# Image sums in four column tiles, an energy split in halves, and half of the attention additions moved behind the roots, in a two-layer kernel on Trainium2

## The chip, the cores and the metric

The kernel runs on one core of one Trainium2 chip, all in float32. The metric is the device time of one launch in microseconds (us), compared between kernels that are timed on the same chip. The kernel before takes 2922.1 us in the median of three runs (2920.12 to 2923.42).

## The reference, cut to what matters

`x` holds 4 sequences (B) of 32 images (T) of 128 x 128. Layer 0 normalises x in groups, treats each of the 32 slices of a sequence as an image and runs a neural operator on it: Fourier-based q, k and v with 32 heads, softmax attention over the 32 images, a projection `p`, and then

```python
a = _inorm(p + xa, attn_w, attn_b)
an = _inorm(a, norm2_w, norm2_b)
m = _fno_layer(an, m0cw, m0sw, H, W, inner_norm=True, act=True)
m = _fno_layer(m, m1cw, m1sw, H, W, inner_norm=True, act=False)
out = _inorm(m, mon_w, mon_b) + a
```

`_inorm` subtracts an image's mean and divides by its standard deviation. `_fno_layer` adds a spectral convolution (a product with weights on 64 x 33 Fourier modes) to a scaled copy of its input; with `inner_norm` the convolution's result is normalised first, and `act` puts a gelu behind it. Layer 1 is an additive attention over 1024 tokens and a mixture of experts; the change doesn't touch it.

## The kernel before, in words

Layer 0 is a loop over the sequences, `for b in range(B)` (from L912), with one pass per b of some 193 us. Its instructions are written in program order for a scheduler that decides the order on each engine; `behind(later, earlier)` (L144) adds a dependence that only orders two instructions. Layer 1 (from L1897) has its order written out by hand.

The stage around the change, in one pass:

- `stats` (L258) turns the statistics of `q` (the attention's projected output plus the input, for 32 images) into a mean and a variance per image; its copy to `flat` (L282) also carries the zero mode. The roots are taken by `inv_std` (L243 on): Ln and Exp on ScalarE (ACT; L248, L251), then four small steps on VectorE (DVE; L252 to L255). From them come `ra`, the factor of q in `a`, and `r2`.
- `spectra` (L1101) transforms 32 images to modes in two halves of 16. In each half TensorE (PE) forms `pz` (L305), DVE or ACT copies it to `z` (L225, L227), PE forms `px` (L1123); ACT squares px (`sqx`, L1125); DVE multiplies px with the weights (`part1`, L1134, and `part2`, L1137); GpSimd (POOL) adds the two into `spec` (L1140); ACT writes a negated copy of a part of it (`negative`, L1085). `part1` and `part2` share a ring of three buffers with the `v1` copies (L356).
- `energy` (L1087) weighs the squares (L1091) and sums them over a row (L1099). For layer 0's first convolution it is called once over both halves by `weighed` (L1150), which makes `v0_s`, has PE sum it over the partitions (`ms`, L383) and copies the result (L1169). `inv_std("r0", ...)` and some small DVE steps then make the scale and the bias of the gelu.
- `row_products` (L334) multiplies one half's `spec` with the inverse transform's columns (`y`, 64 matmuls). `inverse_of` has ACT copy y to `v1` (L356) and PE transform it (`four`, L358). `gelu` (L1208 on) adds q in DVE (`g`, L1212), applies the gelu in ACT (L1216; the first one needs another function table, which is loaded there) and takes statistics in DVE.
- `image_rows` (L389) forms, for the *next* sequence, the sums of x and of x squared over the rows of each image: 32 matmuls (L401, 128 x 512 with 32 columns of weights) that accumulate in `rows8`. x goes to partitions 0 to 31, x squared to 32 to 63, so PE uses two column groups. ACT copies `rows8` (`ev`, L410) and `image_moments` (L413) finishes with 8-row matmuls against an identity. It is called once at the start and once in each of the passes b = 0 to 2; `ms` is ordered behind one of its matmuls, the row products behind its last.
- `add_attention` (L1076) forms `a` in place of x with 8 DVE instructions (L1079) a call, one per image, four calls a pass: 32 instructions, 128 in all. They depend on `q` and `ra` only, and are needed at the pass's end. In the text they come behind the gelus, but having no close consumer they are put by the scheduler wherever DVE is found free.
- `coefficients` (L1274 on) makes the final scales of the pass from two more energies and two roots (`r1`, `rm`). In passes b = 0 to 2 `spectra_of_images` (L482) interleaves it with the preparation of the next sequence's images, where `normed[4]` is the last step of that sequence's scales.

## Time and profile before

| view | what | value |
|---|---|---|
| runs | median of 3 | 2922.1 us |
| the profiled execution | its own time, its span, PE's granted clock | 2926.9 us, 2925.1 us, 0.982 |
| layer 0, layer 1 | stretches of the span | 0 to 835.6 us, 835.6 to 2925.1 us |
| busy share | PE, DVE, ACT, POOL | 94%, 75%, 79%, 70% |
| L1079 | 128 instructions, median of one | 0.341 us |
| L1134, L1137 at b=1 | DVE products of one half | 0.69, 0.68 us |
| L1091, L1099 at b=1 | first energy over 1024 elements | 1.21, 1.21 us |
| L401 at b=1 | 32 image sums, from the first to the end of the last | 365.53 to 373.67 us |
| first gelu | b = 0, 1, 2, 3 | 188.37, 379.89, 571.54, 768.25 us |

The profile is of one execution; its times are read against its own span, and only differences carry over to the median. An engine's busy share is a mean over two very different layers. In a time line a row gives start, duration, engine, line, operation, output and inputs, and in brackets the idle time of the engine just before with the instruction that ended it. Instructions on one engine can overlap by some tenths of a microsecond in these records, so that a chain of equal instructions advances by less than one duration each.

### The profile page before, as it was taken

Reading aid. Unit: us, or ns where it says so; the run is one execution under the profiler, and the core shown is the slowest. Engines: PE = TensorE matmul, PEld = TensorE weight load, DVE = VectorE, ACT = ScalarE, POOL = GpSimd, SP = SyncE. Lnnn points to the kernel's source line nnn. Section 1 sums busy time; section 2 is a strip of 40 time slices with the busy share of each in tenths; the row PEclk is TensorE's granted clock in tenths of the full one; section 3 lists DMA queues with packets and bytes.
Section 4 is the critical chain, followed back from the end, with each engine's and each line's share of the span. In section 5 each row is a group of like instructions: output and inputs, shape, how many; then the busy total and the mean of one; then the engine's idle time right before and its main releaser. Section 6 shows DMA issues by size and latency. Waiting matters only on the chain.

```text
span 2925.1 us, 52645 instructions
## 1 busy us (share of the span) xinstructions
PE 2735.4 (94%) x19506; PEld 1352.7 (46%) x19506; DVE 2189.4 (75%) x4860; ACT 2322.9 (79%) x3243; POOL 2034.0 (70%) x1804
## 2 busy tenths in 40 slices
PE   8898998988878999999899999989999999999997
PEld 5565664655544444334444443434444343444443
DVE  4888788778756777666587787657778776878877
ACT  3556466455469999899899999989999998999991
POOL 1706418146139887878988887898787889798773
PEclk9999999999979999999999999999999999999998
DMA  3304205033020101011000100210000011000000
GB/s 101 123 1 112 78 15 163 13 75 101 19 77 9 25 8 33 8 33 41 19 8 17 24 15 17 49 27 14 24 17 15 19 48 26 15 19 15 15 15 15
DMA packets 151152, 107.71 MB, mean 37 GB/s; under 512 B 36302, under 2 KB 140017, under 8 KB 150897
## 3 DMA queue, kind: packets, MB, share of 16 engines
q1 hardware_dynamic: 147633, 102.26, 13.1%
q8 instruction: 154, 2.52, 0.4%
q10 hardware_dynamic: 3264, 2.10, 0.3%
q14 instruction: 101, 0.83, 0.1%
HBM read 63.86 MB, written 19.50 MB: 28 GB/s over the span
## 4 chain that ended last, share of the span: by engine, by line
PE 47%; POOL 11%; ACT 9%; issue 5%; DVE 5%; DMA 0%; POOLq 0%; SPq 0%; DVEq 0%; ACTq 0%
PE d L1854 20%; PE po L1873 12%; PE px L1760 6%; ACT r L1904 5%; PE n L1854 4%; POOL e L1913 3%; POOL e L1912 3%; ACT e L1920 2%; POOL kx L1519 1%; DVE r L1909 1%; DVE xc L1764 1%; POOL x L1519 1%; PE pl L1738 1%; POOL u L989 1%; ACT r L1916 1%
## 5 line engine op out<-in xcount | busy, mean ns | idle before, releaser
L1909 DVE TENSOR_TENSOR r<-n,r 128x1024 f32<-128x1024 f32 (+1 forms) x1056 | 962.0, 953 | 481.5 <-PE n L1854 397.9
L1912 POOL TENSOR_TENSOR e<-r 128x512 f32<-128x512 f32 x528 | 673.2, 1275 | 273.3 <-DVE r L1909 272.8
L1904 ACT ACTIVATE r<-d 128x1024 f32<-128x1024 f32 (+1 forms) x1056 | 792.9, 802 | 67.4 <-PE n L1854 59.3
L1916 ACT ACTIVATE r<-r 128x1536 f32<-128x1536 f32 x528 | 783.6, 1484 | 16.8
L1913 POOL TENSOR_TENSOR e<-e,r 128x512 f32<-128x512 f32 x528 | 671.3, 1271 | 41.4
L1854 PE MATMUL d<-qe,ke 32*128 32x512 f32 (+3 forms) x2304 | 607.5, 603 | 39.9 <-ACT r L1904 35.8
L1873 PE MATMUL po<-e,kx 128*128 128x512 f32 (+3 forms) x1152 | 594.3, 605 | 17.2 <-POOL e L1925 17.2
L1854 PE MATMUL n<-qe,ke 32*128 32x512 f32 (+3 forms) x2304 | 607.0, 602 | 0.0
L1854 PE MATMUL n<-qf,kf 32*128 32x512 f32 (+3 forms) x2304 | 553.5, 555 | 0.0
L1854 PE MATMUL d<-qf,kf 32*128 32x512 f32 (+3 forms) x2304 | 551.9, 555 | 0.0
L1764 DVE SCALAR_TENSOR_TENSOR xc<-px,wgt,xc 128x128 f32<-128x128 f32 x1024 | 358.4, 351 | 41.4 <-PE px L1760 10.6
L1920 ACT ACTIVATE e<-e 128x512 f32<-128x512 f32 x528 | 325.8, 617 | 66.0 <-POOL e L1913 65.1
L1873 PEld LDWEIGHTS po<-e,kx 128*128 128x128 f32 x1152 | 175.4, 188 | 394.6 <-issue 308.6
L1854 PEld LDWEIGHTS d<-qe,ke 32*128 32x128 f32 x2304 | 177.0, 184 | 360.2 <-ACT r L1904 340.2
L1854 PEld LDWEIGHTS d<-qf,kf 32*128 32x128 f32 x2304 | 220.7, 186 | 177.2 <-issue 164.5
L1760 PE MATMUL px<-we,x2t 128*128 128x512 f32 x512 | 265.9, 605 | 6.8 <-DVE xc L1764 5.5
L989 POOL TENSOR_TENSOR u<-xb,gb 128x858 f32<-128x858 f32 (+1 forms) x112 | 220.5, 2008 | 42.6 <-PE po L926 38.8
L1854 PEld LDWEIGHTS n<-qf,kf 32*128 32x128 f32 x2304 | 228.4, 185 | 18.9 <-issue 11.2
L1140 POOL TENSOR_TENSOR spec<-part,part 128x512 f32<-128x512 f32 x16 | 25.8, 1610 | 286.5 <-DVE gn_r_t L253 93.1
L993 DVE TENSOR_TENSOR u<-xw,gb 128x858 f32<-128x858 f32 (+1 forms) x208 | 215.4, 1100 | 6.8 <-ACT xw L980 3.2
L1854 PEld LDWEIGHTS n<-qe,ke 32*128 32x128 f32 x2304 | 177.9, 183 | 9.4 <-DVE r L1909 0.9
L926 PE MATMUL po<-u,pr 128*32 128x429 f32 (+1 forms) x1280 | 151.2, 532 | 24.9 <-POOL u L989 18.5
(425 smaller groups left out, 3378.4 us busy)
## 6 DMA issues: line engine op xcount, KB each, us to landing
xb<-xd SPq DMA_DIRECT2D x128, 214.5 KB
xc<-x SPq DMA_DIRECT2D x29, 512.0 KB
x<-x SPq DMA_DIRECT2D x16, 512.0 KB
qf<-qe SPq DMA_DIRECT2D x64, 128.0 KB
out<-xc SPq DMA_DIRECT2D x15, 512.0 KB
x<-in_x SPq DMA_DIRECT2D x14, 512.0 KB
xb<-xd SPq DMA_DIRECT2D x32, 198.0 KB
kf<-ke SPq DMA_DIRECT2D x32, 128.0 KB
```

The costliest lines, as they stand in the source:

```text
L989: weighed = nc.gpsimd.tensor_tensor(u, xb, gk, ALU.mult)
L993: weighed_last = nc.vector.tensor_tensor(u, xw, gk, ALU.mult)
L1760: nc.tensor.matmul(px, x2t[:, k * P : (k + 1) * P], we[:, e0 : e0 + 4], start=True, stop=True)
L1764: nc.vector.scalar_tensor_tensor(xc[:, k], px[:, e], wgt[:, k, e0 + e : e0 + e + 1], xc[:, k], ALU.mult, ALU.add)
L1854: nc.tensor.matmul(o, k, q, start=turn == 0 or g > 0, stop=turn == 1 or g > 0)
L1873: nc.tensor.matmul(sums[c, h][:, q0 : q0 + c1 - c0], kx[:, jb], e[:, c0:c1], start=jb == 0, stop=is_last and q0 > 2 * P, skip_group_check= ...
L1904: nc.scalar.activation(r[:, g], d, AF.Ln, scale=1.0 / DSCALE)
L1909: nc.vector.tensor_tensor(r[:, g], part, r[:, g], ALU.mult)
L1912: nc.gpsimd.tensor_tensor(e, r[:, 1], r[:, 2], ALU.add)
L1913: nc.gpsimd.tensor_tensor(e, e, r[:, 0], ALU.add)
L1916: nc.scalar.activation(r, r, AF.Exp, scale=-1.0)
L1920: nc.scalar.activation(e, e, AF.Exp)
```

## The change

Five things change in layer 0.

1. `image_rows` uses four column groups: images of even and odd groups of four go to different 32 partitions, for x and for x squared (`rows8` has 128 partitions). `image_moments` adds the two parts by 64-row matmuls against a new constant `one_row`, made by two DVE additions at the start. Of the sums, all but the first two groups are ordered behind the row products of the first half.
2. The first energy is taken in each half, inside `spectra`.
3. In the second half, the row products of the first half, the image sums, the energy's end (`weighed`) and `ms` are written ahead of `part1` and `part2`; `part1` is ordered behind the step that makes `v0_s` (`roots["by_t"]`). `ms` is ordered behind an image sum that is the eleventh instead of the third from last in the list.
4. Sixteen of the 32 additions are written directly behind `ra` and ahead of `spectra`, which gives them precedence.
5. The other sixteen are written in `coefficients`, behind `normed[4]` (b = 0 to 2), or directly behind `flat` of the gelu's statistics (b = 3).

```diff
--- before.py
+++ after.py
@@ -195,6 +195,11 @@
     one_of_8 = const.tile([P, 39], F32, name="one_of_8")
     nc.vector.memset(one_of_8, 0.0)
     nc.vector.memset(one_of_8[:, 7:8], 1.0)
+    one_row = const.tile([P, 8], F32, name="one_row")
+    for m, i in ((0, 0), (1, 33)):
+        nc.vector.tensor_tensor(
+            one_row[:, m::2], ident[:, i : i + 8 : 2], ident[:, i + 64 : i + 72 : 2], ALU.add
+        )
     ones = const.tile([P, P], F32, name="ones")
     nc.vector.memset(ones, 1.0)
 
@@ -279,7 +284,7 @@
         for r, part in ((0, rows[:, 64:]), (64, rows[:, :64])):
             nc.tensor.matmul(x0[r : r + 64, 1], part, pk[:, 0], start=True, stop=True)
         flat = small.tile([P, 2, T], F32, name="flat", tag="flat")
-        nc.vector.tensor_copy(flat, x0)
+        roots["flat"] = nc.vector.tensor_copy(flat, x0)
         return mean, var, flat
 
     def half_rows(images, z, last):
@@ -348,6 +353,7 @@
                     )
                     for earlier in ahead:
                         behind(mm, earlier)
+        roots["rows"] = mm
         return wide
 
     def four_images(wide, g, copy, v_ring=dict(tag="v", bufs=3), tag="b"):
@@ -386,10 +392,10 @@
     def one(name, n=1):
         return small.tile([P, n], F32, name=name, tag=name)
 
-    def image_rows(xt):
+    def image_rows(xt, earlier=None):
 
         products = []
-        rows8 = ps.tile([64, 4, C], F32, name="rows8", tag="a")
+        rows8 = ps.tile([P, 4, C], F32, name="rows8", tag="a")
         for g in GROUPS:
             xx2 = grp.tile([P, GI, C], F32, name="xx2", tag="pr", bufs=6)
             square = nc.scalar.activation(xx2, xt[:, g : g + GI], AF.Square)
@@ -398,15 +404,18 @@
             for h in range(2):
                 m = g // 4 + h
                 for k, src in enumerate((xt[:, 4 * m : 4 * m + 4], xx2[:, 4 * h : 4 * h + 4])):
+                    r = 64 * k + 32 * (m % 2)
                     mm = nc.tensor.matmul(
-                        rows8[32 * k : 32 * k + 32],
+                        rows8[r : r + 32],
                         one_of_8[:, 7 - m : 39 - m],
                         src,
-                        start=m == 0,
-                        stop=m == 7,
+                        start=m < 2,
+                        stop=m > 5,
                     )
+                    if m > 1 and earlier is not None:
+                        behind(mm, earlier)
                     products.append(mm)
-        ev = grp.tile([64, 4, C], F32, name="ev", tag="pr", bufs=6)
+        ev = grp.tile([P, 4, C], F32, name="ev", tag="pr", bufs=6)
         nc.scalar.copy(ev, rows8)
         return ev, products
 
@@ -415,8 +424,8 @@
         s12 = [ps.tile([P, T], F32, name=f"s{t}", tag="a") for t in "ab"]
         for j in range(4):
             for k in range(2):
-                r = slice(32 * k, 32 * k + 8)
-                nc.tensor.matmul(s12[k][:, j::4], ev[r, j], ident[r, r], start=True, stop=True)
+                r = slice(64 * k, 64 * k + 64)
+                nc.tensor.matmul(s12[k][:, j::4], ev[r, j], one_row[r], start=True, stop=True)
         sv = small.tile([P, 2, T], F32, name="sv", tag="sv")
         for k in range(2):
             nc.vector.tensor_copy(sv[:, k], s12[k])
@@ -1073,12 +1082,17 @@
 
         xr = xt
 
-        def add_attention(g):
+        def add_attention(g, earlier=None):
 
             for t in range(g, g + GI):
-                nc.vector.scalar_tensor_tensor(
+                added = nc.vector.scalar_tensor_tensor(
                     xr[:, t], q[:, t], ra[:, t : t + 1], xr[:, t], ALU.mult, ALU.add
                 )
+                if earlier is not None:
+                    behind(added, earlier)
+
+        for g in GROUPS[:2]:
+            add_attention(g)
 
         def negative(spec, slots):
 
@@ -1098,7 +1112,7 @@
                 behind(product, earlier)
             nc.vector.tensor_reduce(s[:, slots], t, AX.X, ALU.add)
 
-        def spectra(layer, src, ready=(), weights=(), earlier=None):
+        def spectra(layer, src, ready=(), weights=(), earlier=None, between=None):
 
             by_re, by_im = layers[layer][:2]
             spec = big.tile([P, GI, 192], F32, name="spec", tag="spec")
@@ -1125,15 +1139,19 @@
                 nc.scalar.activation(
                     sq[:, 0, s4], px.rearrange("p t r x -> p t (r x)"), AF.Square
                 )
-                if a == 0:
+                if a == 0 or layer == 0:
                     for t, by_row in weights:
                         energy(t, sq, by_row, s4, earlier)
+                if a and between is not None:
+                    between(spec, sq)
                 one_, two = (
                     grp.tile(shape, F32, name=n, tag="v", bufs=3) for n in ("part1", "part2")
                 )
-                nc.vector.tensor_tensor(
+                first_part = nc.vector.tensor_tensor(
                     one_, px, by_re.unsqueeze(1).unsqueeze(1).to_broadcast(shape), ALU.mult
                 )
+                if a and between is not None:
+                    behind(first_part, roots["by_t"])
                 nc.vector.tensor_tensor(
                     two, px[:, :, ::-1], by_im.unsqueeze(1).to_broadcast(shape), ALU.mult
                 )
@@ -1161,7 +1179,9 @@
                 s.rearrange("p (k i) -> p k i", i=2).unsqueeze(2).to_broadcast(spread),
                 ALU.mult,
             )
-            nc.vector.scalar_tensor_tensor(by_t, squares, by_column, by_t, ALU.mult, ALU.add)
+            roots["by_t"] = nc.vector.scalar_tensor_tensor(
+                by_t, squares, by_column, by_t, ALU.mult, ALU.add
+            )
             m = sums("ms", ones, by_t, tag)
             if earlier is not None:
                 behind(summing["ms"], earlier)
@@ -1170,13 +1190,21 @@
             return out
 
 
-        spec, sq = spectra(0, q)
-        ahead = []
-        if b + 1 < B:
-            ev, ahead = image_rows(loaded)
-        v0 = weighed("v0", sq, squares, layers[0][2], "a")
-        if ahead:
-            behind(summing["ms"], ahead[-3])
+        sums_of = small.tile([P, GI], F32, name="v0_r", tag="weighed")
+        wide, between = {}, {}
+
+        def energies(spec, sq):
+
+            wide[0] = row_products(spec, 0)
+            ahead = []
+            if b + 1 < B:
+                between["ev"], ahead = image_rows(loaded, roots["rows"])
+            between["v0"] = weighed("v0", sq, squares, layers[0][2], "a", sums_of)
+            if ahead:
+                behind(summing["ms"], ahead[10])
+
+        spec, sq = spectra(0, q, (), [(sums_of, layers[0][2][0])], None, energies)
+        v0 = between["v0"]
         nc.vector.tensor_mul(v0, v0, r2)
         nc.vector.tensor_mul(v0, v0, r2)
         r0, ve = inv_std("r0", v0)
@@ -1190,7 +1218,7 @@
         nc.vector.tensor_tensor(hb, hb, dq, ALU.add)
         gl = big.tile([P, T, C], F32, name=f"g_{b}", tag="y")
         st = grp.tile([P, T, 6], F32, name="st", tag="st")
-        acts, fours, wide = [], {}, {}
+        acts, fours = [], {}
 
         def in_order(act):
 
@@ -1223,9 +1251,8 @@
                 )
                 nc.vector.bn_stats(st[:, t], gl[:, t])
 
-        wide[0] = row_products(spec, 0, ahead[-1:])
         if b + 1 < B:
-            sv = image_moments(ev)
+            sv = image_moments(between["ev"])
         for g in range(4):
             inverse_of(0, g)
         gelu(0, 0)
@@ -1248,14 +1275,14 @@
         in_order(four_rows([gl[:, 8 + t] for t in range(GI)], early[1], 4, nc.scalar.copy))
         if b + 1 < B:
             summed = group_moments(sv, inverted)
-        for g in GROUPS:
-            add_attention(g)
-
         logarithms()
         if b + 1 == B:
             first((ps, images))
 
         glm, glv, flat = stats("gl", st)
+        if b + 1 == B:
+            for g in GROUPS[2:]:
+                add_attention(g, roots["flat"])
         d1, squares = flat_part(1, flat)
         dg = per_image("dq")
         nc.vector.tensor_copy(dg, d1)
@@ -1300,6 +1327,9 @@
             nc.vector.tensor_mul(dg, dg, c3)
             nc.vector.tensor_tensor(cq, cq, dg, ALU.add)
             made["c2"], made["c3"], made["cq"] = c2, c3, cq
+            if product is not None:
+                for g in GROUPS[2:]:
+                    add_attention(g, normed[4])
 
         if b + 1 < B:
             front = spectra_of_images(b + 1, loaded, normed, coefficients)
```

## The prediction

> **What bounds the kernel now.** I read first the page's busy shares and slices, to see which part of the span the change can reach; then the busy table by stage; then the groups and time lines of the one stage that is touched, in the second pass (b=1); last the chain of waits over the same stage in the last pass. Layer 1 starts at 835.6 us and is untouched, so only the first 835.6 us can move, and what moves there shifts the rest by as much.
>
> The stretch that matters runs, in each of the four passes, from the attention weight `ra` (358.72 at b=1) to the first gelu (379.89). Stage table, columns PE, PEld, DVE, ACT, POOL; the rows are this stage, the b=1 stage between the gelus and the next image's fold, and the last pass's tail:
>
> ```profile
> 354.90:379.90 25.00, 24.31 (x248) 15.92 (x247) 23.01 (x88) 13.15 (x26) 3.46 (x2) 1.00 0.01 2
> 397.40:420.80 23.40, 23.04 (x265) 19.94 (x256) 18.95 (x76) 11.93 (x41) 3.01 (x2) 1.00 0.01 2
> 793.90:816.70 22.80, 16.79 (x153) 11.73 (x153) 16.01 (x56) 5.62 (x13) 2.90 (x2) 0.74 0.18 40
> ```
>
> VectorE (DVE) is 92% busy in the first row: no engine has more of its own to do than DVE and TensorE (PE), and both serve one chain. All 32 additions of the pass lie here (group table, b=1, 358.9 to 379.9):
>
> ```profile
> L1079 DVE SCALAR_TENSOR_TENSOR x<-q,ra,x 128x128 f32<-128x128 f32 x32 | 11.2, 372 | 0.0
> ```
>
> Where they stand decides. Time line of DVE, then POOL, then ScalarE (ACT), b=1:
>
> ```profile
> 359.82 0.34 DVE L1079 SCALAR_TENSOR_TENSOR x<-q,ra,x 128x128 f32<-128x128 f32 x1
> 360.55 0.69 DVE L1134 TENSOR_TENSOR part<-px,mask_rows 128x512 f32<-128x512 f32 x1 [0.39 <-ACT sqx L1125]
> 361.15 0.68 DVE L1137 TENSOR_TENSOR part<-px,turned 128x512 f32<-128x512 f32 x1
> 362.19 1.15 DVE L252 TENSOR_TENSOR r_t<-r 128x32 f32<-128x32 f32 x1 [0.35 <-ACT r L251]
> ...
> 364.34 0.68 DVE L227 TENSOR_SCALAR z<-pz 128x512 f32<-128x512 f32 x1
> ```
> ```profile
> 362.01 1.28 POOL L1140 TENSOR_TENSOR spec<-part,part 128x512 f32<-128x512 f32 x1 [37.40 <-DVE part L1137]
> 369.30 2.18 POOL L1140 TENSOR_TENSOR spec<-part,part 128x512 f32<-128x512 f32 x1 [6.01 <-DVE part L1137]
> ```
> ```profile
> 367.07 0.60 ACT L1125 ACTIVATE sqx<-px 128x512 f32<-128x512 f32 x1 [1.31 <-PE px L1123]
> 371.51 0.42 ACT L1085 ACTIVATE spec<-spec 128x256 f32<-128x256 f32 x1 [3.84 <-POOL spec L1140]
> 373.70 0.58 ACT L410 COPY ev<-rows 64x512 f32<-64x512 f32 x1 [1.77 <-PE rows L401]
> 375.81 0.23 ACT L248 ACTIVATE r<-r_ve 128x32 f32<-128x32 f32 x1 [1.53 <-DVE r_ve L247]
> ```
>
> Only three additions precede `part1`; the rest lie behind, among the small steps of the roots. I call T the end of the second square of px (ACT L1125, 367.67): all later steps need it. After T the last to arrive is PE: the image sums end at 373.70 (ACT waits 1.77 for them), only then comes `ms`, then the root, four v copies, a table load and the gelu at T+12.2. In the last pass, which has no image sums, the chain of waits (745 to 769) goes through DVE instead:
>
> ```profile
> 756.01 1.13 DVE sqx L1091
> 757.14 1.27 DVE x L1079
> 758.41 1.13 DVE v_r L1099
> 759.54 0.26 DVE x L1079
> ```
>
> So additions do sit on the path there, five of them in one 1.27 us piece.
>
> **What the Trainium skill says.** "TensorEngine Tiling (Array Packing)", Available Configurations: an array with 128 rows and 32-column tiles holds four tiles that work independently. The trace agrees in kind: 28 records of po L926, four groups, pass in about 3.0 us, 0.107 us each at 429 columns; the image sums in two groups need 0.43 us a pair. "TensorE: Matmul & The Clock Gate", Step-by-step: only weight loads are pulled ahead, matmuls stay in program order. I use it for a y that waits on POOL and holds px behind it; no row of before shows just that. "SBUF — State Buffer", Who interferes with whom: a DVE operation with two SBUF inputs and a POOL operation that reads SBUF exclude each other. The trace agrees: r_t takes 1.15 instead of 0.18 beside the first POOL addition, and the second POOL addition 2.18 instead of 1.28 beside additions of L1079.
>
> **The change part by part.**
>
> **(1) Sixteen additions straight behind `ra`.** The order in which the two built programs stand on each engine has all 16 ahead of the first half's energy and part1 (before: 1, 3, 6 and 0 of them at b=0 to 3). Back to back they are 0.26 us apart, with a small step of the root between them 0.36. From `ra`'s start at 358.72 they and the small steps fill DVE to about 365.2 (16 x 0.36 is 5.8, and some steps more). Then come the new half energy (0.69 + 0.69, some 0.61 apart), part1 and part2: part2 ends at 367.7 instead of 361.83, and POOL adds 367.75 to 369.0 instead of 362.01 to 363.29. The second half's z copy (DVE, was 364.34) now stands behind part2 too, so it ends about 368.5. And the first y of the row products, which waits for POOL, now stands on PE ahead of the last px matmuls; queued behind it are 12 or more px, and ACT's square waits for those. So px runs 369.3 to 370.4 and T is 371.05: **+3.4**. Likewise +4.5 at b=0, +3.0 at b=2, +4.9 at b=3. Bounds: if the block goes at 0.26 throughout, 16 x 0.26 = 4.2 puts part2 at about 366.0 and T at +1.7; nothing, if something else held T anyway.
>
> **(2) From T to the gelu.** Image sums: 32 records at 0.43 a pair are 6.9 us; four wide at 0.107 they are 3.45, and the 24 that stand behind the row products 2.6. Row products (2.07, was on the path after the sums) are done by about T+1.4. The second energy is 512 wide (0.69 each instead of 1.21), and v_s is ready at T+2.0 instead of T+5.9. Sums done T+4.0, so `ms` no longer waits long. DVE: part2 of the second half follows v_s, ending T+3.2 (was T+1.6); POOL T+3.25 to 4.5, now 1.28 since no additions lie beside it; the negation (0.42) to T+4.95; three v copies (1.54) to T+6.45; ev (0.58, now behind them) to T+6.95; Ln, a v copy, Exp to about T+7.85; the DVE steps without additions between, first g at T+9.65, first gelu about **T+10.2 instead of T+12.2**. The following y at PE, for which ACT waits 1.76 before the next v copy (384.83, T+17.16), comes at T+14.8. So -2.4 at b=0 and 1, -1.6 at b=2 (was T+16.4).
>
> Sum at that copy: b=0 +4.5-2.4 = +2.1; b=1 +1.0; b=2 +3.0-1.6 = +1.4. At b=3 no image sums go, but the additions leave the chain (3.1 us of them in the pieces from 757.1 to 767.8) and the wide energy is halved: about -3.8, so +4.9-3.8 = **+1.1** (+0.3 to +1.4). Four passes: **+5.6**.
>
> **(3) The other sixteen, b=0 to 2**: 16 x 0.34 = 5.4 us go to a stage where DVE has 23.40-18.95 = 4.45 us idle and five stand before the coefficients, eleven among them. They need idle times of 0.73, 0.46, 0.88 us there; the xe and xm products, for which the fold waits, move ahead of the rm chain and gain back what the chain loses. I take +0.2 a pass, **+0.6**; bounds -0.5 (xe alone gains) and +2.9 (11 x 0.26, if all are on the path).
>
> **(4) The other sixteen, b=3**: one block behind `flat` (793.95) and ahead of y0, part1 and part2, 16 x 0.26 = 4.2. Hidden: an idle of 0.90 before dq (waits PE d), and part of the 3.08 before the second part1. Layer 1 waits for this tail. I take **+2.4**, bounds 0 and +4.2.
>
> **(5) Start.** The last image's sums pass after its square (14.06); the rows end at 16.0, ev copies, and the pz chain follows. Two more columns take off about half: **-0.8**, bounds -1.2 and 0. The two DVE additions to build `one_row`, about 0.4 us, lie under the first loads: 0; 0.4 if not. The image sums' order against POOL and SP's queue is unchanged.
>
> Sum: 5.6+0.6+2.4-0.8 = **+7.8**. The profiled execution (2926.9; span 2925.1 and 1.8 around it) becomes 2934.7. It lies 4.8 above the runs' median 2922.1; the same sum on the median gives **2929.9**.
>
> **The rivals.**
> - *Wash.* The block costs 1.7 instead of 3 to 5 a pass (0.26 throughout, small steps slip in). For: it is how x5 in 1.27 looks. Against: b=1's interleaved root steps run at 0.36. 7.8-4x1.7 = +1.0: 2923.1.
> - *Gain, the other side.* Mechanism: T doesn't move, because the block fills DVE's wait for r2's root and for px, while the stage after T keeps its gains. Place: part2 L1137 and z L227. Price: -2.4-2.4-1.6-3.8+0.6+2.4-0.8 = -8.0: 2914.1. It decides where T slips under 2.4 us a pass at b=0 and 1. Against: before part1, DVE's only idle is 0.39, and 0.35 behind part2.
> - *The four tiles don't run four wide.* PE then has 24 records in 5.2, `ms` at T+6.7, and ACT is 0.7 to 1 late: +0.9 on three passes, 2932.6; mostly under ACT's copies.
>
> **How the numbers follow.** Forecast 0.50 (its own range 2925 to 2934, from the bounds of 1 and 4), wash 0.22, gain 0.18, narrow tiles 0.10. About 0.2% (5.8 us, 2916.3 to 2927.9) is what a measurement of this kernel tells from no change. Slower: 0.85 of the forecast, all of narrow, 0.15 of wash: 0.56. Faster: 0.7 of the gain, 0.13. Same 0.31. Range 2917 to 2935: it leaves out most of the gain case and the upper end of (3).
>
> **What would show it.** The first POOL L1140 some 8 to 9 us after `ra` (was 3.3); additions at 0.36, sixteen ahead of L1091; PE idle with POOL as releaser before y; the 24 image sums in about 2.6; T to gelu 10.2; at b=3 a block of sixteen behind L282. Wrong if T slips under 2, if the coefficients' chain is pushed 3 us a pass, or if layer 1 starts before 835.6.

## The result, and the profile after

The changed kernel takes 2940.54 us in the median of four runs (2937.82 to 2944.06), the kernel before 2921.68 beside it: the ratio is 1.0063, with a 95% interval of 1.0051 to 1.0075. So it is slower, by 18.9 us; the forecast had +7.8 and a range up to 2935. The direction was right; the forecast size was less than half of the measured one. The profiled execution after is the longest of the four, 2944.06 (span 2942.3).

Layer 1 begins with ScalarE's table load at 835.55 before and at 856.63 after: layer 0 lost 21.1 us in these two executions. Layer 1, the same code, took 2089.6 and 2085.7, and 2083 to 2090 in the runs below; such differences are not of the change. In what follows the stages of layer 0 are compared, since they are steadier than the whole: in runs in which a stage has the same instructions, most of its times agree within 0.1 us. Two stretches are not steady: the start takes 163.3 to 165.8 in the runs with four column tiles and 164.4 to 166.5 in those with two, and `xe` to the next `ra` at b=2 takes 131.3 to 136.8 over all runs, so that the measured changes of these two rows are within their spread.

All times in us. T is the end of the second square of px of a pass, "copy" the next v copy after the first gelus, `xe` the first fold product of the second stage.

| stage | forecast change (b=0, 1, 2, 3) | measured change | sum forecast | sum measured |
|---|---|---|---|---|
| `ra` to T | +4.5, +3.4, +3.0, +4.9 | +6.22, +4.45, +3.13, +7.91 | +15.8 | +21.7 |
| T to the copy | -2.4, -2.4, -1.6, -3.8 | -1.76, -1.98, -1.21, +0.09 | -10.2 | -4.9 |
| copy to `flat` | 0 | -0.01, -0.02, -0.01, 0 | 0 | 0 |
| `flat` to `xe` | +0.2 each | +0.71, +0.67, +0.60 | +0.6 | +2.0 |
| `xe` to the next `ra` | 0 | -0.23, -0.08, -0.17 | 0 | -0.5 |
| last tail, from `flat` | +2.4 | +3.44 | +2.4 | +3.4 |
| start, to the first `ra` | -0.8 | -0.67 | -0.8 | -0.7 |
| all | | | +7.8 | +21.1 |

The block is where it was forecast. DVE's time line at b=1, after (`ra` stands at 362.98 now), then POOL's and PE's:

```profile
364.08 1.40 DVE L1088 SCALAR_TENSOR_TENSOR x<-q,ra,x 128x128 f32<-128x128 f32 x5
...
368.41 1.14 DVE L1088 SCALAR_TENSOR_TENSOR x<-q,ra,x 128x128 f32<-128x128 f32 x4
369.46 0.69 DVE L1105 TENSOR_TENSOR sqx<-sqx,energy 128x512 f32<-128x512 f32 x1
...
371.26 0.68 DVE L1155 TENSOR_TENSOR part<-px,turned 128x512 f32<-128x512 f32 x1
371.86 0.68 DVE L232 TENSOR_SCALAR z<-pz 128x512 f32<-128x512 f32 x1
```
```profile
372.11 1.26 POOL L1158 TENSOR_TENSOR spec<-part,part 128x512 f32<-128x512 f32 x1 [43.16 <-DVE part L1155]
```
```profile
366.57 1.06 PE L1137 MATMUL px<-z,cst 128*32 128x256 f32 x20
...
373.43 0.48 PE L347 MATMUL y<-cst,spec 32*128 32x128 f32 x2 [2.29 <-POOL spec L1158]
373.84 1.89 PE L1137 MATMUL px<-z,cst 128*32 128x256 f32 x24
```

POOL's addition ends 10.39 us after `ra`; the forecast said 10.28. PE then waits 2.29 us at a y for POOL, with the last 24 px behind it, also as forecast. The next row was not: those 24 px take 1.89, though 20 such records took 1.06 seven us earlier. The busy table of stages (seventh number: PE's granted clock) says why:

```profile
370.00:373.40 3.40, 1.07 (x8) 0.16 (x8) 3.40 (x7) 0.02 (x1) 1.26 (x1) 1.00 0.00 0
373.40:378.00 4.60, 4.57 (x78) 3.65 (x82) 2.06 (x7) 1.01 (x2) 0.00 (x0) 0.63 0.00 0
```

PE came out of its wait at half its clock. At b=3 the wait is longer and the half clock lasts. PE's time line there, after, and then the table from the wait to the copy:

```profile
764.50 1.94 PE L1137 MATMUL px<-z,cst 128*32 128x256 f32 x24 [4.22 <-DVE z L232]
766.37 1.65 PE L310 MATMUL pz<-cst,q 128*128 128x128 f32 x6
...
777.72 3.78 PE L364 MATMUL four<-v,cst 128*128 128x512 f32 x4 [2.97 <-ACT v L362]
...
783.41 2.04 PE L364 MATMUL four<-v,cst 128*128 128x512 f32 x2 [0.32 <-DVE g L1240]
```
```profile
764.00:772.20 8.20, 7.70 (x70) 4.86 (x74) 2.54 (x6) 0.97 (x2) 1.27 (x1) 0.50 0.00 0
772.20:774.70 2.50, 2.50 (x58) 2.32 (x54) 2.32 (x5) 0.04 (x1) 0.00 (x0) 0.78 0.00 0
774.70:777.70 3.00, 0.05 (x1) 0.00 (x0) 2.42 (x6) 0.93 (x3) 1.26 (x1) 0.84 0.00 0
777.70:782.00 4.30, 4.29 (x12) 1.75 (x16) 1.29 (x8) 3.06 (x6) 0.00 (x0) 0.50 0.01 4
782.00:790.30 8.30, 7.99 (x68) 4.49 (x60) 6.09 (x26) 3.21 (x9) 0.00 (x0) 0.50 0.00 0
```

In the kernel before, the same stage of b=3 was at half clock from 760.5 to about 767 only. The image sums do run four wide: of the 24 behind the row products, four start every 0.43 us (at b=1 four from 378.44 to 378.46, the next from 378.90 on), where before two did. (These are records: each float32 matmul of the program stands as two records in these traces, so that the "32 matmuls" of the image sums are 16 of the program.)

The tail has the block of sixteen behind `flat`, and nothing hides it except 0.9 us:

```profile
811.59 0.23 DVE L287 COPY flat<-x 128x64 f32<-128x64 f32 x1 [1.17 <-PE x L285]
811.73 4.29 DVE L1088 SCALAR_TENSOR_TENSOR x<-q,ra,x 128x128 f32<-128x128 f32 x16
...
818.76 0.68 DVE L1155 TENSOR_TENSOR part<-px,turned 128x512 f32<-128x512 f32 x1
```

### The profile page after: what moved, and what is told of

Read it like the earlier page. It is cut to its first block, busy times and chain, and to the rows that moved or that the text cites. A ratio compares the mean times of both kernels' runs of the same rounds, so it can differ in the third digit from the quotient of the medians.

```text
span 2942.3 us, 52647 instructions
## 1 busy us (share of the span) xinstructions
PE 2729.9 (93%) x19506; PEld 1347.5 (46%) x19506; DVE 2188.1 (74%) x4870; ACT 2321.8 (79%) x3243; POOL 2033.2 (69%) x1804
## 4 chain that ended last, share of the span: by engine, by line
PE 48%; POOL 14%; ACT 10%; DVE 6%; issue 6%; DMA 0%; POOLq 0%; SPq 0%; DVEq 0%; ACTq 0%
PE d L1884 20%; PE po L1903 11%; PE px L1790 6%; ACT r L1934 5%; POOL e L1942 4%; POOL e L1943 4%; PE n L1884 3%; ACT e L1950 2%; POOL kx L1549 2%; POOL x L1549 2%; DVE r L1939 2%; POOL u L998 1%; DVE xc L1794 1%; PE po L935 1%; PE pl L1768 1%
## 5 line engine op out<-in xcount | busy, mean ns | idle before, releaser
L1884 PEld LDWEIGHTS n<-qf,kf 32*128 32x128 f32 x2304 | 228.0, 185 | 19.3 <-issue 12.2
```

The costliest lines, as they stand in the source:

```text
L1884: nc.tensor.matmul(o, k, q, start=turn == 0 or g > 0, stop=turn == 1 or g > 0)
```

## The experiments

Two theories stood at first. **A**: the block behind `ra` makes the kernel slow, and the rest of the change gains. **B**: the loss is spread over the other parts. A third came from the result: **A2**, that a good part of what the forecast missed is PE's clock, which falls after PE's own idle stretches. Each experiment gives its ratio to the kernel before, timed beside it, with the 95% interval, and then its stages. Medians of different experiments are not compared directly.

### The change without the block

```diff
-        for g in GROUPS[:2]:
-            add_attention(g)
         def negative(spec, slots):
...
+        for g in GROUPS[:2]:
+            add_attention(g)
         logarithms()
```

> The changed kernel without its first step: the first sixteen additions of each pass are written where they were before, behind the gelus, so that they fill VectorE's idle times; everything else of the change stays. Theory A (the block of sixteen behind ra is what makes the kernel slow: it pushes T, the end of the second square, by 22 us over four passes): T comes back to within 1 us a pass of before and the shorter stage behind it remains, so 8 to 12 us faster than the kernel before, about 2912. Rival B (the loss is spread over the other moved additions, the image sums and the split energy): still 8 to 15 us slower than before, about 2933.

Measured: 1.0020 (1.0013 to 1.0027), +5.2 us. T comes back to before at b=1 and 2 (`ra` to T 8.81 and 10.07), not at b=0 and 3 (12.81 and 10.34; 9.64 and 8.78 before). T to the copy is 15.4 to 15.6 everywhere. But the copy-to-`flat` stretch grows by 0.64 in three passes and 1.18 in the last (ScalarE waits for a pz at its end; why was not pursued), `flat` to `xe` keeps its +0.7, and the tail +2.95. So A holds for the block, without which most of the loss is gone, and fails for the rest, which doesn't make the kernel faster.

### The block alone, in the kernel before

```diff
+        for g in GROUPS[:2]:
+            add_attention(g)
         def negative(spec, slots):
...
-        for g in GROUPS:
+        for g in GROUPS[2:]:
             add_attention(g)
```

> The kernel before with one part of the change alone: sixteen additions of each pass are written directly behind ra, ahead of the spectra; the other sixteen stay fillers. Theory A: T slips by 3 to 6 us a pass as in the changed kernel, and sixteen fewer fillers behind T give back 1 to 2 a pass, so 10 to 15 us slower than before, about 2934. Rival B: the block hides in idle times of VectorE, within 3 us of before. The variant of A in which a y that waits for POOL and stands ahead of px is needed for the slip: less than 8 us slower, as the row products are not moved here.

Measured: 1.0034 (1.0021 to 1.0046), +8.7 us. T slips by 5.46, 2.47, 0.96 and 5.88, and T to the copy gives back 1.48, 1.34, 0.01 and 2.62. That is a little short of A's 10 to 15. The moved row products aren't needed for most of the slip at b=0 and 3. At b=1 and 2 the changed kernel has 2 us more; 1.2 of them are the half energy ahead of part2 (POOL's addition ends 9.0 to 9.2 after `ra` here, 10.2 to 10.4 there).

### The second sixteen of the last pass back as fillers

```diff
-        if b + 1 == B:
-            for g in GROUPS[2:]:
-                add_attention(g, roots["flat"])
...
+        if b + 1 == B:
+            for g in GROUPS[2:]:
+                add_attention(g)
         logarithms()
```

> The changed kernel, but in the last pass the second sixteen additions are fillers behind the gelus again, not a block behind flat. Theory: the stretch from flat to layer 1 (41.6 us before, 45.0 us changed) comes back to 41.6 to 42, some 3 us less than the changed kernel, so about 15.5 us slower than before. Rival (the tail is held by TensorE's clock, which was at half there before too): the stretch stays at 44 to 45 us and the time at that of the changed kernel, about 19 us slower than before.

Measured: 1.0050 (1.0037 to 1.0062). The tail is 41.92 instead of 45.04, as the theory says: its block costs 3.1 us. One thing was not in anybody's account: with the same instructions from T to the copy, b=3 took 14.91 there in this run and 18.03 in the changed kernel. Here the half clock behind the second wait was over sooner: it lasted from 772.4 to 779.2, in the changed kernel from 776.7 to 790.4. How long PE stays at half differs from one execution to the next. The clock records of all 18 kept traces show in what way: the clock changes only in whole steps of 3.41 us (two steps here, four there), and the grid of these steps is fixed within an execution and lies otherwise in each.

### Extra products in PE's idle stretches

```diff
+            for i in range((0, 2, 2, 0)[b]):
+                extra = nc.tensor.matmul(between["wide"][0][:, i % 2], ident, q4, start=True, stop=True)
+                behind(extra, roots["pz"])
...
+            if b == 3:
+                idle = ps.tile([P, 4, C], F32, name="idle", tag="b")
+                for i in range(3):
+                    extra = nc.tensor.matmul(idle, ident, q[:, :4], start=True, stop=True)
+                    behind(extra, summing["ms"])
```

(`q4` stands for the first four images of q as one row; the row products take over the two tiles of `between["wide"]`.)

> The changed kernel with extra matmuls whose results nobody reads, put into stretches in which TensorE sat idle: two of 128x512 behind the last pz of the second half at b=1 and 2, three behind ms at b=3 (idle of 2.97 us, after which the granted clock was 0.5 until 790). Theory A2 (the half clock follows TensorE's own idle stretches, and the part of the loss that the forecast missed, some 4 us at b=3 and 1 us at b=1, is that clock): clock near 1 in the stretch from ms to the second row products at b=3, 3 to 5 us less than the changed kernel. Rival B2 (the clock is granted for other reasons): the clock stays at 0.5 there and the time stays or grows by 1 to 3 us, for the extra work.

Measured: 1.0052 (1.0039 to 1.0064). At b=3 the extra products leave 0.40 us of idle ahead of `four`; the clock is 1.00 from the wait on, T to the first gelu is 8.79 instead of 10.28, and T to the copy 14.04 instead of 18.03. At b=1 `ra` to T is 12.61 instead of 13.40. PE's line at b=3 behind the unread products:

```profile
771.28 1.98 PE L366 MATMUL four<-v,cst 128*128 128x512 f32 x4 [0.40 <-ACT v L364]
```

The extra work made things faster, as A2 says. How much at b=3 is less sure: the run before this one and the one with two column groups have the changed kernel's instructions from T to the copy and took 14.91 without the fill, so it is worth 0.9 to 4.0 there; the first gelu stood at T+10.28 in all of these, and comes 1.5 earlier. (At b=2 the order of y and px changed as well, so that its 1.2 us don't count.)

### No moved additions: items 1 to 3 alone

```diff
-        for g in GROUPS[:2]:
-            add_attention(g)
...
+        for g in GROUPS:
+            add_attention(g)
         logarithms()
...
-                add_attention(g, roots["flat"])
...
-                    add_attention(g, normed[4])
```

> The changed kernel without its moved additions: all 32 of a pass are fillers written behind the gelus as before; the image sums in four tiles, the split energy and the earlier row products stay. The run without the block kept 3 us in the last tail and 0.7 us a pass in the second stage; if those belong to the second sixteen they go, and 16 more fillers lie between T and the gelu. Theory A (moved additions carry the loss): within 3 us of before, 2920 to 2925. Rival B (image sums, energy and row products as they stand cost something themselves): 6 us or more slower than before, 2928 or above.

Measured: 1.0041 (1.0029 to 1.0054), and so not theory A: the image sums, the split energy and the early row products, with the additions as fillers, cost about as much as the block alone. T to the copy is 19.16, 20.85, 19.02 and 15.84 (17.19, 17.16, 16.39, 17.94 before). DVE at b=1, then PE:

```profile
374.59 6.62 DVE L1088 SCALAR_TENSOR_TENSOR x<-q,ra,x 128x128 f32<-128x128 f32 x21
...
381.23 0.18 DVE L1186 COPY v<-ms 128x32 f32<-128x32 f32 x1
```
```profile
381.56 0.35 PE L428 MATMUL sa<-one_row,ev 64*128 64x8 f32 x1 [3.39 <-DVE v L1186]
```

`ms` was issued at 375.95; its copy stands behind 21 additions until 381.23. PE meanwhile sits idle for 3.39 us and comes out at half clock (0.50 from 379 to 389). The chain is shorter, so the additions no longer have gaps between its steps, and stand in front of one step instead. As much of the loss lies ahead of T: `ra` to T is 12.81 at b=0 and 13.27 at b=3 (9.64 and 8.78 before). There a y waits for POOL (1.42 and 1.38 us) and holds pz and px behind it, and part of what follows is at half clock; in the run with the second half late, where y stands behind px, the two are 10.66 and 9.41.

### y behind px

```diff
-            wide[0] = row_products(spec, 0)
+            wide[0] = row_products(spec, 0, [roots["px"]])
```

(`roots["px"]` is the last px matmul of the half.)

> The changed kernel with one order added: the first half's row products (y) stand behind the last px of the second half on TensorE. Theory (with the block there, y waits for POOL and holds px behind it): T slips 1.5 to 2 us less at b=1, about 1 less at b=2, at most 0.5 less at b=0 and 3, where y stood in the middle of px and its data were there; 3 to 4 us less than the changed kernel. Rival (px waits for VectorE's z copy, which stands behind part2 as well, or for the clock): less than 1 us, as the changed kernel.

Measured: 1.0052 (1.0039 to 1.0064). `ra` to T is 15.62, 11.36, 12.00 and 14.96: less by 0.24, 2.04, 1.25 and 1.73 than in the changed kernel. The wait at y that holds px is real at b=1 and 2. At b=2 neither run is at half clock, and its 1.25 is the order's alone. At b=1 some 0.8 of the 2.04 is the clock: PE's wait is 1.44 instead of 2.29 here, the clock stays at 1.00, and the 24 px take 1.08 instead of 1.89. So the order is worth 1.2 in each, at b=1 less than the 1.5 to 2 expected. At b=3 the clock again came back sooner, so that its 1.7 us aren't the order's alone.

### Two column groups again

```diff
-        rows8 = ps.tile([P, 4, C], F32, name="rows8", tag="a")
+        rows8 = ps.tile([64, 4, C], F32, name="rows8", tag="a")
...
-                    r = 64 * k + 32 * (m % 2)
+                    r = 32 * k
```

(The start and stop flags and the 8-row products against the identity are as before, too.)

> The changed kernel with the image sums in two column groups again (rows8 of 64 partitions, 8-row products against the identity), everything else as changed. The 24 sums behind the row products take 5.2 instead of 2.7 us, so ms comes 2.5 us later. Theory (they are on the path from T to the gelu, with less than 1 us of slack behind ScalarE's copies): T to the gelu 1.5 to 2.5 us longer at b=0 to 2, so 4 to 7 us slower than the changed kernel. Rival (ScalarE's negation and copies hide them): within 1.5 us of the changed kernel.

Measured: 1.0077 (1.0065 to 1.0090). T to the first gelu is 12.96, 11.22 and 11.24 against 10.37 each: 2.6, 0.85 and 0.87. Four tiles are worth 4.3 us in the stage here, the sum at the lower end of what the theory gave. At b=0, where all the sums stand behind the row products, `ms` comes 3.4 later and 2.6 of it show; at b=2 it comes 2.6 later and 0.87 show: ScalarE's negation and copies hide the rest. Ahead of T the slower sums give something back at b=1, where `ra` to T is 12.60 instead of 13.40. The first eight sums take longer, PE's wait is 1.44 instead of 2.29, and the clock stays at 1.00:

```profile
376.24 0.48 PE L347 MATMUL y<-cst,spec 32*128 32x128 f32 x2 [1.44 <-POOL spec L1158]
376.65 1.08 PE L1137 MATMUL px<-z,cst 128*32 128x256 f32 x24
```

That is the px in 1.08 instead of 1.89, with only the width of the sums changed, and the same `ra` to T as with the two unread products.

### The additions as fillers, with the last pass kept at full clock

As the run without moved additions, with three extra products behind `ms` at b=3.

> As e5_no_moved_additions, with three extra unread matmuls of 128x512 behind ms at b=3, where TensorE is idle and the granted clock has been 0.5 after it in the kernel before and in the changed one. Theory A2 (the clock follows the idle stretch): clock 1 there and 1 to 3 us less than e5. Rival: equal to e5, or 1 us more if the extra products stand in the way of four.

Measured: 1.0049 (1.0036 to 1.0063), no faster than without them. The first gelu comes 11.04 after T instead of 11.27, but the copy 19.64 instead of 15.84: PE waited 2.27 us for g from 776.7 on, and the clock was at 0.50 from 777.7 to 788. To fill one wait moved the fall to the next one. This neither supports nor breaks A2; it shows that a fill has to cover every wait.

### The second sixteen behind the coefficients

On the changed kernel: y behind px, the first sixteen as fillers, and

```diff
-            if product is not None:
-                for g in GROUPS[2:]:
-                    add_attention(g, normed[4])
+            for g in GROUPS[2:]:
+                add_attention(g, last)
```

(`last` is the last step on `cq`; the block behind `flat` is gone.)

> The changed kernel's image sums, split energy and row products (these behind px), the first sixteen additions as fillers, the second sixteen behind the last step of the coefficients in every pass, the last one included. Theory (in the run without the block what was lost came from the second sixteen: 0.7 us a pass among the coefficients' steps, 3 us ahead of part2 in the last tail): second stage back to 21.5 to 21.7 up to xe, the tail at 41.6 to 42.5, so 3 to 5 us less than the run without the block, at or up to 3 us below the kernel before. Rival (sixteen additions cost their 4 us wherever they stand, since VectorE is full): 4 us or more slower than before.

Measured: 1.0013 (1.0006 to 1.0019), +2.9. `flat` to `xe` is back at 21.4 to 21.7, as the theory said, but the additions are paid elsewhere: `xe` to the next `ra` is 1.4 us longer at b=0 and b=1, and the tail 45.84. The rival is nearer: sixteen additions in a row are 4.2 us of DVE, and nowhere in the stages tried are they free.

### Three extra products in the kernel before

```diff
+        if b == 3:
+            idle = ps.tile([P, 4, C], F32, name="idle", tag="b")
+            for i in range(3):
+                extra = nc.tensor.matmul(idle, ident, q[:, :4], start=True, stop=True)
+                behind(extra, roots["px"])
         v0 = weighed("v0", sq, squares, layers[0][2], "a")
```

> The kernel before with one thing added: three unread matmuls of 128x512 behind px of the last pass, in the 4.67 us for which TensorE waits for v_s there and behind which its granted clock was 0.5 for 6.6 us. Theory A2 (the clock follows the idle stretch): clock 1 from ms on; two of the first four products run at 1.12 instead of 1.9 us each, so the first gelu 1 to 2 us earlier, 1 to 2 us less than before. Rival (an idle of some 1.3 us that remains is enough, or the clock has other reasons): within 0.5 us of before.

Measured: 0.9999 (0.9990 to 1.0007). Of the idle of 4.67 us ahead of `ms`, 2.58 remained, and the clock still fell to 0.50. Inconclusive on A2: the fill was too short.

### The four column tiles alone

The kernel before with `rows8` over 128 partitions and `one_row`; nothing else.

> The kernel before with the four column tiles alone (rows8 of 128 partitions, one_row); energy, row products and additions as before. The sums end 3.5 us earlier, but v_s, which ms needs too, was ready only 0.1 us ahead of their end. Theory (the split energy is what lets the sums' gain through): T to the first gelu 0 to 0.7 us shorter a pass, 0 to 2 us less than before in all, plus up to 0.8 at the start. Rival (the sums were the path, row products behind them included): 2 us a pass, 6 to 8 us less than before.

Measured: 1.0016 (1.0008 to 1.0024): slower by 4.2 us, which neither side had expected from a change that only makes PE's work shorter. T to the first gelu at b=0 to 2 is 13.25, 14.66 and 14.64 (12.2 before). PE at b=1 and the table:

```profile
371.54 0.45 PE L388 MATMUL ms<-v_s,ones 128*128 128x32 f32 x2 [2.50 <-DVE v_s L1172]
371.92 2.52 PE L347 MATMUL y<-cst,spec 32*128 32x128 f32 x40
```
```profile
369.00:372.00 3.00, 0.51 (x10) 0.43 (x6) 2.92 (x8) 0.89 (x2) 0.33 (x1) 0.95 0.00 0
372.00:375.00 3.00, 3.00 (x46) 2.78 (x48) 2.97 (x16) 0.98 (x4) 0.00 (x0) 0.50 0.02 5
375.00:378.00 3.00, 3.00 (x14) 1.99 (x15) 2.13 (x14) 1.04 (x3) 0.00 (x0) 0.50 0.00 0
378.00:381.00 3.00, 3.00 (x10) 1.22 (x9) 2.12 (x8) 2.68 (x5) 0.00 (x0) 0.50 0.00 0
```

The sums end early, v_s isn't ready, PE is idle for 2.50 us, and the row products and the `four` behind it run at half clock. In the kernel before, the slow sums filled just this wait.

### The tiles alone, with the last pass filled

As the last run, with the three extra products of the run before it.

> The four column tiles alone and the three unread matmuls of the last pass together. If both theories hold, the gains add: 1 to 4 us less than before, the best version so far. Rival: the same as the better of the two alone.

Measured: 1.0022 (1.0012 to 1.0032), no better than the tiles alone: the waits of the first three passes are not filled, and the three products don't cover that of the last.

### The tiles alone, with the wait filled

```diff
+        if ahead:
+            idle = ps.tile([P, 4, C], F32, name="idle", tag="b")
+            for i in range(3):
+                extra = nc.tensor.matmul(idle, ident, q[:, :4], start=True, stop=True)
+                behind(extra, ahead[-1])
         v0 = weighed("v0", sq, squares, layers[0][2], "a")
```

> The run with the four column tiles alone, plus three unread matmuls of 128x512 behind the last image sum at b=0 to 2, where TensorE sat idle for 2.50 us until v_s came and its granted clock was 0.5 for some 10 us behind. Theory A2 (that idle stretch, made by the faster sums, brings the half clock, and the half clock the loss): clock 1 through the stage, T to the first gelu at b=1 from 14.7 to about 12, b=2 likewise, 4 to 6 us less than the tiles alone, at the kernel before or 2 us below. Rival (the order of ms, y and the v copies that comes with early sums causes it): T to the gelu stays above 13.5 and the time within 1.5 us of the tiles alone, or above it for the extra work.

Measured: 0.9992 (0.9984 to 1.0000); the tiles alone were at 1.0016. T to the first gelu is 12.29, 12.37 and 12.38. The idle ahead of `ms` at b=1 is 0.19, and the clock stays at 1.00 (the three unread matmuls stand as six records):

```profile
366.77 2.84 PE L1188 MATMUL idle<-q,ident 128*128 128x512 f32 x6
369.55 0.48 PE L347 MATMUL y<-cst,spec 32*128 32x128 f32 x2
370.22 0.38 PE L388 MATMUL ms<-v_s,ones 128*128 128x32 f32 x2 [0.19 <-DVE v_s L1172]
```
```profile
369.00:372.00 3.00, 2.81 (x58) 2.06 (x60) 2.96 (x15) 0.06 (x1) 0.00 (x0) 1.00 0.02 5
372.00:375.00 3.00, 3.00 (x42) 2.05 (x34) 3.00 (x17) 2.29 (x6) 0.00 (x0) 1.00 0.00 0
```

More work on PE, and the whole loss is gone. That settles A2 for this stage. Its median is also the lowest of all, 2919.69 beside 2921.62, but with an interval that ends at 1 it is not told from the kernel before.

### The last pass of the kernel before, filled

As the run with three extra products in the kernel before, but with six.

> The kernel before with six unread matmuls behind px of the last pass; with three, 2.58 us of idle were left ahead of ms and the clock still fell to 0.5. Theory A2: with less than 1 us left the clock stays at 1, the first gelu comes 1 to 2 us earlier than before and the run is 1 to 2 us shorter. Rival: the clock falls there whatever stands ahead of it, the time is that of before.

Measured: 1.0000 (0.9992 to 1.0008). With 0.66 us left ahead of `ms` the clock stays at 1.00 and the first gelu comes 11.70 after T instead of 13.56, as A2 says. But PE then waits 1.65 for g, is at half clock from 764.2 to 767.6, and the copy comes at 18.60 (17.94 before). The mechanism is confirmed, the gain is given back.

### Three passes changed, the last as before

The run with the second half late, with b=3 as in the kernel before:

```diff
+        if b + 1 < B:
             spec, sq = spectra(0, q, (), [(sums_of, layers[0][2][0])], None, energies)
+        else:
+            spec, sq = spectra(0, q)
+            v0 = weighed("v0", sq, squares, layers[0][2], "a")
...
+        else:
+            wide[0] = row_products(spec, 0)
```

(All 32 additions of b=3 are fillers.)

> The best of the parts: at b=0 to 2 the image sums in four tiles, the split energy, row products behind px, sixteen additions as fillers and sixteen behind the coefficients (the run with the second half late); at b=3, which has no image sums, the pass as it stood before. Theory (the first three passes gained 3 us and the last gave back 4, nearly all in its tail): b=3 takes 89.6 us from ra again instead of 93.7, so 3 to 4 us less than the run with the second half late, 0 to 3 us below the kernel before. Rival (the gain of three passes is spread of the start and of one long stage, 357 to 743, not of the change): as before or up to 3 us slower.

Measured: 1.0002 (0.9993 to 1.0010). b=3 is back at 89.6 us from `ra`; the 0.7 to 1.7 us a pass that the stage from `ra` to the copy gains go into the stretch behind `xe`, 0.8 to 1.8 longer. A wash.

### The same, with the last pass filled

The six extra products at b=3 added to the last run.

> As e15_three_passes, with the six unread matmuls of e14_before_filled at b=3. If the clock theory holds, 1 to 2 us less than e15; if not, equal to e15.

Measured: 1.0000 (0.9992 to 1.0008), as without them; b=3 repeats the run with six (first gelu at T+11.70, copy at T+18.60).

## Why the prediction was right and wrong

**Right**: what bounds the stage, the place of the sixteen additions, and their first consequence. POOL's addition ended 10.2 to 10.4 us after `ra` at b=0 to 2 (forecast 10.28 at b=1), y held px at b=1 and 2, the sums took 2.8 us four wide (forecast 2.6), the first gelu came 10.37 after T (forecast 10.2). The start's -0.67 (forecast -0.8) is within its spread and shows nothing.

**Wrong, step (1)**, "px runs 369.3 to 370.4 and T is 371.05": the px, and at b=0 and 3 the pz between them, were priced at the speed of before. They ran at half clock, behind the wait that the forecast itself had made for PE (2.29 at b=1, 2.99 at b=0, 4.22 at b=3). By the rows: at b=0, 24 px in 1.94 instead of some 1.1 and 6 pz in 1.65 instead of some 0.8, 1.7 in all, which is that pass's miss (6.22 against 4.5); at b=1 0.8 for px and 0.2 for y, against a miss of 1.05; at b=3 3 us. At b=2 PE's wait at y was 1.16 us, the clock stayed at 1.00, and there the forecast hit (3.13 against 3.0):

```profile
566.77 0.48 PE L347 MATMUL y<-cst,spec 32*128 32x128 f32 x2 [1.16 <-POOL spec L1158]
```

By these durations the whole 5.9 us of this step is the clock. Other runs show it at b=1 alone: with that wait shortened by unread products or by slower sums, `ra` to T was 12.61 and 12.60, beside a forecast of 12.3. At b=0 and 3 no run filled the wait ahead of px, and there it is read from the durations only.

**Wrong, step (2)** at b=3, "about -3.8", measured +0.09: the shortened chain was there (relative to T, `ms` 3.7 us and the first gelu 3.3 us earlier), but the row products and `four` behind a second wait of 2.97 ran at half clock until 790. With that wait filled the stage is 14.04, a gain of 3.9, as forecast. The size of this loss depends on the execution: 18.03 in the changed kernel's profile, 14.91 in two other runs with the same instructions. At b=0 to 2 the gain was smaller by 0.4 to 0.6 each, 0.2 of it ahead of the gelu and the rest between the gelu and the copy. It is not `ms`: that came at T+4.8 at b=0 and 1 and at T+4.0, as forecast, at b=2, with the first gelu at T+10.37 each time.

**Mis-sized, steps (3) and (4)**: +2.0 instead of +0.6, +3.4 instead of +2.4. In (3) I let `xe`'s new place pay for the additions; at b=1 it stands behind all sixteen on DVE all the same. In (4) the 3.08 us ahead of the second part1 hid nothing, since what filled it (POOL, y, px) was itself behind the block. This size, too, varies: the tail took 44.55 to 45.73 in the five runs with this block behind `flat`.

Of the 13.3 us between +7.8 and +21.1, 5.9 lie in step (1), 5.3 in step (2), 1.4 and 1.0 in (3) and (4).

**The rivals.** The wash case priced the block at 1.7 us a pass; alone it moved T by 14.8 in all. The gain case had the wrong trigger: not only the block but the rest, too, loses when the additions go back to the gaps (1.0041). The case of tiles that don't run four wide is refuted. None of the cases had the clock, though the page's own figures show it: 0.74 in the stage table's tail row, which I quoted, and 0.5 at b=3 in the kernel before. The Trainium skill has it too: "TensorE: Matmul & The Clock Gate", What's actually happening, says that PE's clock is halved after an idle window of about 3.4 us, in windows that run freely, and comes back after a busy one. The traces agree in kind (0.50 and 1.00) and in the step (every stretch at half clock lasts a whole multiple of 3.41 us, on a grid that lies otherwise in each execution). They differ in what is enough for a fall: at b=1 of the changed kernel PE was busy for a third of the step ahead of it (1.06 us of 3.35 from 370.55 on), and an idle stretch of 1.65 us was followed by half clock in one run, while one of 1.79 us in another was not.

**What stays open**: how the loss of the changed kernel divides into waits and clock over many executions, since only one of each was profiled; how much of the loss ahead of T at b=0 and 3 a filled wait would give back; and what load of PE in a step decides. PE's busy share alone doesn't: the clock fell behind a step with 85% (379.9 to 383.3 in the run with the second sixteen of the last pass as fillers) and stayed at 1.00 behind one with 46% (266.3 to 269.7 in the run without moved additions).

## What to carry to other kernels

When a change makes PE wait, or makes PE's work end sooner, ask for how long it will be idle and price what follows it at half clock too; a faster step that only lengthened a wait, to 2.50 us here, made the kernel slower. Fillers in the gaps of a chain are free only as long as the chain has these gaps: shorten the chain, and the same instructions stand in front of its next step. Read the granted clock by stage, in the kernel before as well, ahead of every sum, and in more than one execution: the same instructions took 14.91 or 18.03 us here.

## What the runs showed of the hardware

- PE's granted clock went from 1.00 to 0.50 behind idle stretches of 1.65, 2.27, 2.29, 2.50, 2.58, 2.97, 3.39 and 4.22 us, and stayed at 1.00 behind 0.19, 0.40, 0.66, 1.16, 1.44 and 1.79. This gives no threshold: at b=0 of the changed kernel it also fell at 189.6, with PE busy for 2.82 of the 3.40 us before and no idle stretch over 0.34.
- In all 18 kept traces the clock is 0.50 or 1.00 and changes only on a grid of 3.41 us, which lies otherwise in each execution. In the stages shown here the half clock lasted 3.41 to 13.65 us.
- Three matmuls of 128x512 that nobody reads (2.84 us) in each of three passes made the kernel with four column tiles 0.24% faster by the ratios (1.0016 to 0.9992).
- Four column tiles: four 128x512 records with 32 columns of weights start within 0.02 us and the next four 0.43 later, against two in 0.43 with two groups.
